# The rests of A as float16 against the bfloat16 upper halves of the weights, in the second product of a gated block

## The chip, the cores and the metric

The kernel runs on one core of a Trainium2 chip. The metric is the device time of one execution in microseconds (us). Before the change it is 698.72 us, the median of three runs (698.67 to 698.84).

## The reference

A block of two gated products over x (2 x 1024 tokens x 2048). The first multiplies the layer-normalised x, quantised to 8 bits, with a quantised context. The second multiplies the layer-normalised result with a 0/1 weight matrix of 2048 x 2048. Cut to what matters:

```python
x = x + tanh(g_xattn[0]) * matmul(fake_quant(layernorm(x)), fake_quant(ctx_4096))

y = layernorm(x)                                # 2 x 1024 x 2048
y_ei = concatenate([y[..., :1638], -4.0 * y[..., 1638:]], -1)
out = einsum('bsi,if->bsf', y_ei, kernel.astype(float32))   # kernel: 2048 x 2048, true or false
x = x + tanh(g_ffn[0]) * scale * out
```

Everything is float32 in the reference. The change concerns the second product alone.

## The kernel before

**Tiles and stages.** The 2048 tokens are 16 tiles of 128. The first half of the kernel's work on a batch (8 tiles) is the first product; its operands are small whole numbers held in float16 (matmuls at lines 544 and 646; line 574 makes a column sum of the context with a matrix of ones). The second product follows, batch by batch. It works on *pairs* of token tiles (p, 8 of them) as a 2 x 2 block product: A is split into four blocks (two token tiles, two halves of the 2048 inputs), the weights B into four blocks of 1024 x 1024, and a scheme with seven block products (M1 to M7) instead of eight combines sums and differences of the blocks. `ops_product2(q, ...)` handles two pairs at a time (q = 0 to 3), and for them goes through the seven products in the order of `ORDER`.

**One product for one pair.** The left block is 128 tokens x 1024 inputs, that is KH = 8 steps k of 128 inputs; the right block is 1024 wide, in two halves j of 512. To keep float32's accuracy the left block A is split in two:

- `part_hi` (line 738, ACT) copies A into a page of type fp32r, which keeps fewer bits of the fraction. This is `hi`.
- `part_lo` (line 742, DVE or POOL, as the planner chooses) takes the difference A - hi, also as fp32r. This is `lo`, the rest.

The weights lie in memory as bytes; `load_w` brings them in, and `widen` (line 782, ACT) turns 1024 of them per partition into fp32r, one page for each step k. They are whole numbers of small size.

`mm2` (line 809) then issues, for each k, four matmuls into the same accumulator in PSUM: hi with the left and the right half of the weights, lo with the left and the right half. The 128 x 128 piece of hi or lo is the stationary operand, which is loaded into TensorE's array before each matmul; the 512 columns of weights are the moving operand. There are 4 x 7 x 2 x 8 x 4 = 1,792 such matmuls, 896 with hi and 896 with lo. For an fp32r matmul the load of the stationary operand is part of the matmul instruction; for float16 it is an instruction of its own in TensorE's queue. The profile shows loads of both kinds as rows of the engine PEld.

After the last k of a product, `add2` (line 825, DVE) adds the accumulator, times the factor `f2`, onto the old x, and `store2` writes it out.

**Where A comes from.** `factor` (lines 447 to 461, DVE) makes one over the standard deviation for each tile; `scale2` (line 685, DVE) applies it; `turn2` (line 692, TensorE) transposes four pieces of 128 x 128 at a time, in float32, and `take2` copies them to A. `combine` (lines 722 to 728) forms the block sums.

**Order.** All engines' instructions are written out in an order that a planner makes: every piece of work is an `op` with a cost per engine, the buffers that it needs and a due time; `Plan.order` simulates them and keeps the best of two tries. TensorE's main work stands in a fixed order, and transposes and column sums are put in between. The two pairs of a product are staggered by LAG = 4 steps of k: four steps of the first pair, then steps of the two in turn, then four steps of the second.

Of the kernel before, what the change touches and what calls it, by code (L numbers as in the profile page):

```python
# [12 lines left out]
F32R = mybir.dt.float32r  # L13
F16 = mybir.dt.float16
BF = mybir.dt.bfloat16
# [3 lines left out]
ALU = mybir.AluOpType  # L19

P = 128
NB = 512
HB = 1024
EPS = 1e-5
UNIT = 2.0**-24
CENTER = 128.0
PAGES = 44

# [6 lines left out]
class Plan:  # L35
# [77 lines left out]
    def order(self, lag, start, runs, seed=1):  # L113


        self.dues()
        chance = random.Random(seed)
        free, count = dict(self.free), dict(self.count)
        dues = [o.due for o in self.ops]
        best = None  # L120
        for i in range(runs):
            self.free, self.count = dict(free), dict(count)
            try:
                end = self.run(lag, start)
            except RuntimeError:
                end = None
            if end is not None and (best is None or end <= best[0]):
                best = end, self.began, [o.engine for _, _, o in self.began]
                dues = [o.due for o in self.ops]
                held = self.held_up()  # L130
            for o, due in zip(self.ops, dues):
                o.due = due
            for ops in held:
                if chance.random() < 0.5:
                    step = chance.choice((3.0, 6.0, 12.0, 24.0))
                    for o in ops:
                        o.due -= step
            if i % 3:
                place = chance.uniform(0.0, self.place)
                for o in self.ops:  # L140
                    if o.place is None and abs(o.due - place) < 120.0 and chance.random() < 0.1:
                        o.due += chance.uniform(-25.0, 25.0)
        _, self.began, engines = best
        for (_, _, o), e in zip(self.began, engines):
            o.engine = e
        return [o for _, _, o in self.began]
# [133 lines left out]
def gated_xattn_ffn_kernel(  # L280
# [26 lines left out]

    nc = tc.nc  # L310
    B, S, D = x.shape
    K = kv.shape[1]
# [7 lines left out]
    KH = KT // 2  # L320
# [19 lines left out]
    def page(shape, dtype, name: str):  # L340
        return pages.tile([P] + shape, dtype, tag="page", name=name)
# [8 lines left out]
    sc = const.tile([P, 7], F32, name="sc")  # L350
    nc.sync.dma_start(sc, scalars.partition_broadcast(P))
    gate = const.tile([P, 2], F32, name="gate")
# [8 lines left out]
    c1 = const.tile([P, 1], F32, name="c1")  # L361
    nc.vector.tensor_scalar(c1, z1, -1.0, CENTER, ALU.mult, ALU.add)
    c2 = const.tile([P, 1], F32, name="c2")
# [3 lines left out]
    f1u = const.tile([P, 1], F32, name="f1u")  # L367
    nc.vector.tensor_scalar(f1u, f1, 1.0 / UNIT, None, ALU.mult)
    f1c1u = const.tile([P, 1], F32, name="f1c1u")
# [7 lines left out]
    nc.vector.tensor_scalar(kc12d, f1c1, c2, float(K), ALU.mult, ALU.mult)  # L377
    nc.vector.tensor_scalar(kc12, c1, -CENTER, None, ALU.add)
    nc.vector.tensor_scalar(kc12, kc12, f1c2, float(K), ALU.mult, ALU.mult)
    f2 = const.tile([P, 1], F32, name="f2")  # L380
    nc.vector.tensor_scalar(f2, gate[:, 1:2], sc[:, 6:7], None, ALU.mult)

    ident = const.tile([P, P], F32, name="ident")
    make_identity(nc, ident)
# [56 lines left out]
    def factor(v, t: int):  # L441


        va, sd = root.pop((v, t))
        mean = mv[v, t][:, 0:1]
        r0 = small.tile([P, 1], F32, tag="r0", name=f"r0_{v}{t}")
        nc.vector.reciprocal(r0, sd)

        e = small.tile([P, 1], F32, tag="e", name=f"e_{v}{t}")
        nc.vector.tensor_scalar(e, r0, r0, va, ALU.mult, ALU.mult)  # L450
        nc.vector.tensor_scalar(e, e, -0.5, 1.5, ALU.mult, ALU.add)
        r = small.tile([P, 1], F32, tag="r", name=f"r_{v}{t}", bufs=T)
        nc.vector.tensor_scalar(r, r0, e, None, ALU.mult)
        fac[v, t] = (r, mean)
        if v == "a":
            w = small.tile([P, 1], F32, tag="w", name=f"w_{v}{t}")
            nc.vector.tensor_scalar(w, va, r, zs1, ALU.mult, ALU.mult)
            nc.vector.tensor_scalar(w, w, mean, None, ALU.subtract)
            nc.vector.tensor_scalar(r, r, rs1, None, ALU.mult)
            wr = small.tile([P, 1], F32, tag="wr", name=f"wr_{v}{t}")  # L460
            nc.vector.tensor_scalar(wr, w, r, None, ALU.mult)
            fac[v, t] = (r, w, wr)
# [42 lines left out]
    def take1(t: int, h: int, engine=None):  # L505
# [5 lines left out]
        if engine == "ACT":  # L511
            nc.scalar.activation(dst, v, AF.Copy, bias=-CENTER)  # L512
        else:
            nc.vector.tensor_scalar(dst, v, -CENTER, None, ALU.add)  # L514

# [159 lines left out]
    A, hi, lo, wt, wb, wr, wf, back, acc2 = ({} for _ in range(9))  # L675
# [54 lines left out]
    def left(m: str, p: int):  # L730

        t, u = 2 * p, 2 * p + 1
        return {"M1": (t, 0), "M2": (t, 1), "M3": (t, 1), "M4": (u, 1), "M5": (u, 0),
                "M6": (t, 0), "M7": (p, "S3")}[m]
# [3 lines left out]
        nc.scalar.copy(hi[m, p], A[left(m, p)])  # L738

    def part_lo(m: str, p: int, engine=None):  # L740
        lo[m, p] = page([KH, P], F32R, f"lo_{m}_{p}")
        engines[engine].tensor_sub(lo[m, p], A[left(m, p)], hi[m, p].bitcast(F32))  # L742


# [51 lines left out]
    def apart(p: int, m: str):  # L796

        return p == T // 2 - 1 and SUM[m] == "Y"

    def mm2(q: int, m: str, p: int, k: int, js=(0, 1)):  # L800
        if m in OPENS and k == 0 and apart(p, m):
            acc2[SUM[m], p] = [ps_tr.tile([P, NB], F32, tag="tr", name=f"acc2_{m}_{p}_{j}") for j in range(2)]
        elif m in OPENS and k == 0:
            acc = ps_acc.tile([P, 2, NB], F32, tag="acc", name=f"acc2_{m}_{p}")
            acc2[SUM[m], p] = [acc[:, j, :] for j in range(2)]
            acc2[SUM[m], p, 0] = flat(acc)
        for part in (hi, lo):
            for j in js:
                nc.tensor.matmul(  # L809
                    acc2[SUM[m], p][j],  # L810
                    part[m, p][:, k, :],
                    wf[q, m, k][:, ts(j, NB)],
                    start=(m in OPENS and k == 0 and part is hi),
                    stop=(k == KH - 1 and part is lo),
                    skip_group_check=True,
                )
# [17 lines left out]
    def ops_norm(v: str, t: int, **when):  # L834
        name = lambda kind: ((kind + v, t), 0)
        op({"DVE": 2.0}, variance, v, t, writes=[name("v")], **when,
           reads=[(("bn" + v, t), c) for c in range(NC)])
        op({"ACT": 1.0}, square_root, v, t, reads=[name("v")], writes=[name("sd")], **when)
        op({"DVE": 8.0 if v == "a" else 4.0}, factor, v, t, reads=[name("sd")], writes=[name("r")], **when)
# [187 lines left out]
    def ops_parts(m: str, p: int):  # L1027
        a = ("A",) + left(m, p)
        op({"ACT": ACT(HB)}, part_hi, m, p, reads=both(a), writes=[(("hi", m, p), 0)],
           opens=[("page", ("hi", m, p))], lead=60)  # L1030
        op({"DVE": DV2(HB), "POOL": GPS(HB)}, part_lo, m, p, reads=[*both(a), (("hi", m, p), 0)],
           writes=[(("lo", m, p), 0)], opens=[("page", ("lo", m, p))], lead=60, port=True)
# [20 lines left out]
    def ops_product2(q: int, between):  # L1053
        pairs = (2 * q, 2 * q + 1)
        for n, m in enumerate(ORDER):
# [27 lines left out]
            for i, k, *js in steps:  # L1083
                p = pairs[i]
                js = js[0] if js else (0, 1)
                acc = ("acc2", SUM[m], p)
                two = apart(p, m)
                keys = [(acc + (j,), 0) if two else (acc, j) for j in js]
                opens = [("tr", acc + (j,)) for j in js] if two else [("acc", acc)]
                op({"PE": 2.1 * len(js)}, mm2, q, m, p, k, js, main=True, writes=keys,  # L1090
                   reads=[(("hi", m, p), 0), (("lo", m, p), 0), (("wf", q, m, k), 0)],
                   opens=opens if m in OPENS and k == 0 else [])
                if k == KH - 1:
                    for js2 in [(j,) for j in js] if two else [js]:
                        v = ("back", p) + TAKES[m]
                        keys = [(acc + (j,), 0) if two else (acc, j) for j in js2]
                        op({"DVE": DV2(len(js2) * NB)}, add2, m, p, js2, reads=keys, writes=[(v, j) for j in js2],
                           due=plan.place)
                        if m in LAST:
                            op({"SP": DMA}, store2, p, *TAKES[m], js2, reads=[(v, j) for j in js2], due=plan.place + 60)  # L1100
# [67 lines left out]
    for t in range(TPB, T):  # L1168
        v = ("x", t, 1)
# [60 lines left out]
```

## Time and profile before

| | |
|---|---|
| time, median of three | 698.72 us |
| time of the profiled execution | 698.79 us |
| its span in the profile | 697.0 us |
| granted TensorE clock | full |
| TensorE matmul busy | 674.0 us |
| TensorE weight load busy (beside the matmuls) | 471.7 us |
| VectorE (DVE) busy | 490.2 us |
| ScalarE (ACT) busy | 455.4 us |
| GpSimd (POOL) busy | 316.8 us |
| DMA | 155.78 MB |
| second product, first batch | about 145 to 367 us of the span |
| second product, second batch | about 476 to 693 us |

In a row of the profile's groups stand the line, the engine, the operation, the tile that it writes and those that it reads, the shape, the count, then the busy time, the mean length of one in ns, and the idle time of the engine before them with what ended it. Matmuls overlap: the length of one runs from its start to the end of its results, which is longer than the distance to the next one. The timeline gives start and length in us and an engine's row; neighbours of the same kind are merged (x2). In the chain of work that ended last each row has a start, a length and what ran.

### The profile page before, as it was taken

Reading aid. Unit: us, or ns where it says so; the run is one execution under the profiler, and the core shown is the slowest. Engines: PE = TensorE matmul, PEld = TensorE weight load, DVE = VectorE, ACT = ScalarE, POOL = GpSimd, SP = SyncE. Lnnn points to the kernel's source line nnn. Section 1 sums busy time; section 2 is a strip of 40 time slices with the busy share of each in tenths; the row PEclk is TensorE's granted clock in tenths of the full one; section 3 lists DMA queues with packets and bytes.
Section 4 is the critical chain, followed back from the end, with each engine's and each line's share of the span. In section 5 each row is a group of like instructions: output and inputs, shape, how many; then the busy total and the mean of one; then the engine's idle time right before and its main releaser. Section 6 shows DMA issues by size and latency. Waiting matters only on the chain.

```text
span 697.0 us, 8833 instructions
## 1 busy us (share of the span) xinstructions
PE 674.0 (97%) x3180; PEld 471.7 (68%) x3180; DVE 490.2 (70%) x717; ACT 455.4 (65%) x536; POOL 316.8 (45%) x210
## 2 busy tenths in 40 slices
PE   1999999989999999999999999999999999999997
PEld 0444444468788888878885444447888888888885
DVE  6899958899998886497878888468572425583331
ACT  4599444286888566699926768229699347689540
POOL 8166789863625221855717887975120101040000
PEclk9999999999999999999999999999999999999999
DMA  8999406777995799477379677327074379155032
GB/s 302 393 393 380 162 13 231 259 261 251 361 400 225 233 324 339 140 247 278 120 263 330 222 268 245 121 92 275 27 260 162 105 231 324 67 170 222 22 131 90
DMA packets 63580, 155.78 MB, mean 223 GB/s; under 512 B 4912, under 2 KB 21296, under 8 KB 63536
## 3 DMA queue, kind: packets, MB, share of 16 engines
q1 hardware_dynamic: 63536, 155.21, 62.9%
q8 instruction: 25, 0.41, 0.2%
q14 instruction: 19, 0.16, 0.1%
HBM read 117.44 MB, written 37.75 MB: 223 GB/s over the span
## 4 chain that ended last, share of the span: by engine, by line
PE 87%; DMA 4%; DVE 4%; POOL 2%; ACT 2%; issue 1%; SPq 0%; ACTq 0%; DVEq 0%
PE acc_M L809 57%; PE acc L544 19%; PE acc_M L646 7%; PE tr L692 4%; DMA kv<-in_kv_dram 3%; DMA x<-in_x_dram 1%; POOL x L596 1%; DVE wB L767 1%; ACT wf_M L782 1%; POOL x L592 1%; PE tr L503 1%; DVE qn L472 0%; PE cs L574 0%; DVE x L685 0%; DVE bn_b L426 0%
## 5 line engine op out<-in xcount | busy, mean ns | idle before, releaser
L809 PE MATMUL acc_M<-wf_M,hi_M 128*128 128x512 f32 x896 | 282.0, 395 | 1.6 <-ACT wf_M L782 1.5
L809 PE MATMUL acc_M<-wf_M,lo_M 128*128 128x512 f32 x896 | 277.6, 390 | 0.6 <-POOL lo_M L742 0.6
L782 ACT ACTIVATE wf_M<-wr_M 128x1024 fp32r<-128x1024 uint8 x224 | 221.6, 1050 | 26.8 <-DMA wr_M<-in_wmask_dram 24.2
L809 PEld LDWEIGHTS acc_M<-wf_M,lo_M 128*128 128x128 f32 x896 | 168.0, 188 | 36.8 <-POOL lo_M L742 1.3
L809 PEld LDWEIGHTS acc_M<-wf_M,hi_M 128*128 128x128 f32 x896 | 164.1, 188 | 34.4 <-ACT wf_M L782 3.2
L544 PE MATMUL acc<-q,q1T 128*128 128x512 f16 x768 | 171.6, 381 | 1.2 <-DVE q1T L514 0.8
L825 DVE SCALAR_TENSOR_TENSOR back<-acc_M,f,back 128x1024 f32<-128x1024 f32 (+1 forms) x58 | 72.1, 1245 | 124.7 <-PE acc_M L809 117.1
L742 POOL TENSOR_TENSOR lo_M<-A,hi_M 128x1024 fp32r<-128x1024 f32 x24 | 62.1, 2586 | 179.5 <-ACT hi_M L738 160.1
L544 PEld LDWEIGHTS <-q1T 128*128 128x128 f16 x768 | 75.2, 98 | 90.2 <-issue 1.9
L592 POOL TENSOR_TENSOR x<-x,row 128x512 f32<-128x512 f32 x64 | 88.6, 1408 | 43.8 <-ACT sd_a L438 15.5
L596 POOL TENSOR_TENSOR x<-x,e 128x512 f32<-128x512 f32 x64 | 92.0, 1458 | 30.6 <-ACT e L586 16.1
L738 ACT CAST hi_M<-A 128x1024 fp32r<-128x1024 f32 x48 | 50.1, 1044 | 13.1 <-POOL A L726 4.7
L530 ACT ACTIVATE q<-kv,sc,rs 128x1024 uint8<-128x1024 f32 x45 | 53.5, 1236 | 7.8 <-DMA kv<-in_kv_dram 5.1
L586 ACT ACTIVATE e<-acc,tokb,f1u 128x512 f32<-128x512 f32 x34 | 25.1, 774 | 49.6 <-PE acc L544 47.8
L426 DVE BATCH_NORM_STATS2 bn_b<-x 128x6 f32<-128x512 f32 x64 | 43.1, 684 | 15.9 <-POOL x L596 15.6
L495 ACT COPY A<-tr 128x512 f32<-128x512 f32 x35 | 20.3, 584 | 46.5 <-PE tr L692 45.8
L742 DVE TENSOR_TENSOR lo_M<-A,hi_M 128x1024 fp32r<-128x1024 f32 x24 | 33.7, 1421 | 7.2 <-ACT hi_M L738 7.2
L568 DVE TENSOR_TENSOR pair<-pair,q 128x1024 f16<-128x1024 f16 x36 | 36.6, 1022 | 2.5 <-ACT q L530 0.8
L728 POOL TENSOR_TENSOR A<-A,A 128x1024 f32<-128x1024 f32 x8 | 21.1, 2648 | 23.7 <-DVE A L726 16.4
L522 POOL MEMSET q<- 128x1024 f32 x32 | 29.2, 952 | 5.1 <-DVE q L532 2.2
L512 ACT ACTIVATE q1T<-tr 128x1024 f16<-128x1024 uint8 x22 | 21.3, 1019 | 7.5 <-PE tr L503 6.8
L767 DVE SCALAR_TENSOR_TENSOR wB<-wB,wB 128x2048 uint16<-128x2048 uint16 x8 | 24.2, 3031 | 0.0
(103 smaller groups left out, 594.1 us busy)
## 6 DMA issues: line engine op xcount, KB each, us to landing
kv<-in_kv_dram SPq DMA_DIRECT2D x64, 512.0 KB, 9.2
x<-in_x_dram SPq DMA_DIRECT2D x32, 512.0 KB, 7.7
x<-x SPq DMA_DIRECT2D x32, 512.0 KB, 3.0
back<-x SPq DMA_DIRECT2D x32, 512.0 KB, 6.1
wr_M<-wt_T SPq DMA_DIRECT2D x32, 512.0 KB, 5.6
out_dram<-back SPq DMA_DIRECT2D x30, 512.0 KB, 3.6
wr_M<-in_wmask_dram SPq DMA_DIRECT2D x24, 512.0 KB, 5.4
n<-in_x_dram SPq DMA_DIRECT2D x16, 512.0 KB, 7.2
```

The costliest lines, as they stand in the source:

```text
L426: nc.vector.bn_stats(bn[v, t][:, c, :], xt[src[v, t, c // 2]][:, ts(c % 2, NB)])
L530: nc.scalar.activation(low, v, AF.Identity, bias=z2, scale=rs2)
L544: nc.tensor.matmul(acc1[b, c, tiles[0]][:, i, :], q1T[tiles[i]][:, k, :], rhs1(b, c, k), start=(k == 0), stop=(k == KT - 1),)
L568: nc.vector.tensor_add(colsum[b, c], colsum[b, c], v[:, i : i + 2, :])
L592: nc.gpsimd.tensor_add(xc, xc, colrow[b, c])
L596: nc.gpsimd.tensor_add(xc, xc, ev.pop((t, c)))
L646: nc.tensor.matmul(acc1[key][:, i, :], left_half(p, LEFT1[m])[:, 4 * s + k, :], right1(m, h, s)[:, k, :], start=(m in OPENS and s == 0 and ...
L738: nc.scalar.copy(hi[m, p], A[left(m, p)])
L742: engines[engine].tensor_sub(lo[m, p], A[left(m, p)], hi[m, p].bitcast(F32))
L782: nc.scalar.activation(wf[q, m, k], wr[q, m, k // 4][:, k % 4, :], AF.Copy, bias=-float(RIGHT[m][1]))
L809: nc.tensor.matmul(acc2[SUM[m], p][j], part[m, p][:, k, :], wf[q, m, k][:, ts(j, NB)], start=(m in OPENS and k == 0 and part is hi), stop= ...
L825: nc.vector.scalar_tensor_tensor(v, acc, f2, v, ALU.mult, ALU.add)
```

## The change

`lo` becomes a page of float16, in `part_lo`. Its matmuls no longer read the widened weights as fp32r but the upper 16 bits of each as bfloat16, that is every second 16-bit element of the same page. The hi matmuls stay as they were. So that the small rests lie in float16's range, A is scaled by 2^19 in the factor of the second normalisation (`factor`, for v = "b"), and `f2` is divided by 2^19. In the planner, a list is given a first value; no cost is changed.

```diff
+BIG = 2.0**19
...
-        best = None
+        best, held = None, []
...
-    nc.vector.tensor_scalar(f2, gate[:, 1:2], sc[:, 6:7], None, ALU.mult)
+    nc.vector.tensor_scalar(f2, gate[:, 1:2], sc[:, 6:7], 1.0 / BIG, ALU.mult, ALU.mult)
...
-        nc.vector.tensor_scalar(e, e, -0.5, 1.5, ALU.mult, ALU.add)
+        big = BIG if v == "b" else 1.0
+        nc.vector.tensor_scalar(e, e, -0.5 * big, 1.5 * big, ALU.mult, ALU.add)
...
     def part_lo(m: str, p: int, engine=None):
-        lo[m, p] = page([KH, P], F32R, f"lo_{m}_{p}")
+        lo[m, p] = page([KH, P], F16, f"lo_{m}_{p}")
         engines[engine].tensor_sub(lo[m, p], A[left(m, p)], hi[m, p].bitcast(F32))
...
-        for part in (hi, lo):
+        w = wf[q, m, k]
+
+        upper = w.bitcast(BF).rearrange("p (n b) -> p n b", b=2)[:, :, 1]
+        for part, rhs in ((hi, w), (lo, upper)):
             for j in js:
                 nc.tensor.matmul(
                     acc2[SUM[m], p][j],
                     part[m, p][:, k, :],
-                    wf[q, m, k][:, ts(j, NB)],
+                    rhs[:, ts(j, NB)],
                     start=(m in OPENS and k == 0 and part is hi),
```

In the new file line 809 is line 817, and line 742 is line 747.

## The prediction

> **What bounds the kernel now.** First the page's busy shares and the chain that ended last:
>
> ```profile
> PE 674.0 (97%) x3180; PEld 471.7 (68%) x3180; DVE 490.2 (70%) x717; ACT 455.4 (65%) x536; POOL 316.8 (45%) x210
> PE 87%; DMA 4%; DVE 4%; POOL 2%; ACT 2%; issue 1%; SPq 0%; ACTq 0%; DVEq 0%
> PE acc_M L809 57%; PE acc L544 19%; PE acc_M L646 7%; PE tr L692 4%; DMA kv<-in_kv_dram 3%; DMA x<-in_x_dram 1%; POOL x L596 1%; DVE wB L767 1%; ACT wf_M L782 1%; POOL x L592 1%; PE tr L503 1%; DVE qn L472 0%; PE cs L574 0%; DVE x L685 0%; DVE bn_b L426 0%
> ```
>
> TensorE makes 87% of the chain, and line 809, the line of the change, 57% of the span, 397 us. Then the groups:
>
> ```profile
> L809 PE MATMUL acc_M<-wf_M,hi_M 128*128 128x512 f32 x896 | 282.0, 395 | 1.6 <-ACT wf_M L782 1.5
> L809 PE MATMUL acc_M<-wf_M,lo_M 128*128 128x512 f32 x896 | 277.6, 390 | 0.6 <-POOL lo_M L742 0.6
> L809 PEld LDWEIGHTS acc_M<-wf_M,lo_M 128*128 128x128 f32 x896 | 168.0, 188 | 36.8 <-POOL lo_M L742 1.3
> L544 PE MATMUL acc<-q,q1T 128*128 128x512 f16 x768 | 171.6, 381 | 1.2 <-DVE q1T L514 0.8
> L544 PEld LDWEIGHTS <-q1T 128*128 128x128 f16 x768 | 75.2, 98 | 90.2 <-issue 1.9
> ```
>
> The two matmul groups of line 809 wait only 1.6 + 0.6 us in all, so the stage is bound by how fast TensorE strings its matmuls together. The means of 395 and 381 ns are latencies that overlap; the price of a matmul is the distance to the next. From the chain in order of time:
>
> ```profile
> 439.29 29.35 PE acc L544 x136
> 506.40 70.77 PE acc_M L809 x312
> 615.45 77.13 PE acc_M L809 x340
> ```
>
> float16: 29.35 / 136 = 215.8 ns each. fp32r: 70.77 / 312 = 226.8 and 77.13 / 340 = 226.9 ns. Over all 1,792 matmuls of line 809 the distances in the records average 227.7 ns once the six real stalls (over 250 ns) are left out; the 0.9 ns above 226.8 sit in some ten matmuls after each stall or transpose (230 to 236 ns), 1.8 us in all.
>
> **The change, part by part.** The programs built from both versions carry the same work in the same order on every engine and queue, with the same number of waits: planner costs are untouched and the extra `held = []` only matters if a first plan fails. One thing differs: each of the 896 `lo` matmuls now has a weight load that is an instruction of its own, as line 544 has; an fp32r matmul has its load built in.
>
> *The bare widths.* 896 `lo` matmuls from 226.8 to 215.8 ns would take off 896 x 11.0 = 9.9 us (9.7 with 226.7 and 215.9; I use 9.7). All of it would lie on the path: the waits of line 809 are 2 us, and the second batch's first product, which follows at 367 us, waits 0.3 us once (line 646 for ACT).
>
> *The joint between the two kinds.* After the change, every k step of a pair runs hi, hi, lo, lo: fp32r, fp32r, f16, f16, 448 such groups. The trace of before holds this pattern once, where the column sum of line 574 stands inside the second product (TensorE's rows, then its weight loads; start and length in us):
>
> ```profile
> 351.07 0.62 PE L809 MATMUL acc_M<-wf_M,hi_M 128*128 128x512 f32 x2
> 351.52 0.61 PE L809 MATMUL acc_M<-wf_M,lo_M 128*128 128x512 f32 x2
> 351.98 0.61 PE L574 MATMUL cs<-pair,ones_h 128*128 128x512 f16 x2
> 352.24 0.81 PE L809 MATMUL acc_M<-wf_M,hi_M 128*128 128x512 f32 x2
> 352.89 0.62 PE L809 MATMUL acc_M<-wf_M,lo_M 128*128 128x512 f32 x2
> ```
>
> ```profile
> 351.30 0.41 PEld L809 LDWEIGHTS acc_M<-wf_M,lo_M 128*128 128x128 f32 x2
> 351.98 0.12 PEld L574 LDWEIGHTS <-ones_h 128*128 128x128 f16 x2 [0.26 <-issue]
> 352.21 0.41 PEld L809 LDWEIGHTS acc_M<-wf_M,hi_M 128*128 128x128 f32 x2
> ```
>
> From 351.98 to 352.89, two f16 and two fp32r matmuls take 0.91 us. Two and two at their own widths would be 0.432 + 0.454 = 0.886; four fp32r take 0.907. So the joint eats what the narrower matmuls give. The weight loads say where: an fp32r load starts together with the matmul before it, while the f16 load waits until the last fp32r matmul has streamed (351.98, the very start of its own matmul). In the records' nanosecond stamps the ends of the matmuls (start plus length) follow each other by 232 and 216 (f16), then 229, 233, 231, 227 (fp32r). The other joint of this kind, from line 809 into line 646 at 366.95 us, gives the same 232, then 215 and 216. A new group is thus 232 + 216 + 229 + 233 = 910 ns, against 4 x 227.7 = 910.8 on average now: 448 x (910 - 910.8) = -0.4 us.
>
> Here the Trainium skill speaks otherwise. "TensorE: Matmul & The Clock Gate", in its spec table and in "Architectural detail", has the queue pull weight loads ahead of matmuls in flight; "Weight-path perf modes" has the load fast for 128 columns of a type other than FP32. The fast load shows (98 against 188 ns). By the pulling ahead, f16 behind fp32r would cost 216, and the sum would be the 9.7 us of the bare widths. The two joints measured show no pulling ahead of a separate load past an fp32r matmul, so I take 910. Bounds: if the fp32r pair keeps to an undisturbed 227, the group is 232 + 216 + 227 + 227 = 902 (-3.9 us); if the first f16, coming after a disturbed fp32r matmul, takes the 238 ns that is the worst seen after a transpose, it is 916 (+2.3 us).
>
> *The moving operand at every second bfloat16.* No TensorE row of before reads with a step. The nearest is the fp32r row itself: it streams the same 2 KB per partition in 226.8 ns, so a step of two need not cost more than that, 11 ns over the contiguous f16. Bounds: 0, by the page "SBUF — State Buffer", section Door 1, whose rule is that at least two hits on a 16-byte line are read at full bandwidth (here four); and, if only half of the columns came per cycle, as much again as a matmul, 896 x 0.213 = 191 us. I take 0: bytes and lines are the fp32r row's, and 2 KB in 227 ns was shown.
>
> *Line 742, the rest in float16.* 24 on POOL at 2,586 ns, 24 on DVE at 1,421, and 8 more. The inputs stay f32, so I take no change. Half the written bytes might save some (the f16-only DVE sums of lines 628 and 630 take 1.05 to 1.49 us for the same 1,024 elements); a dearer conversion could cost. Cover: POOL waits 160.1 us at this line for the hi copies, and TensorE waits 0.6 + 1.3 us for lo. Without that cover, each 0.1 us more costs at most 56 x 0.1 = 5.6 us, which needs every one on the path.
>
> *The rest*: the scaling by 2^19 rides on instructions that exist (one more scalar in f2, about 0.2 us at the start, used only from the first add of the second product on; other constants in line 451). Pages, DMAs and buffers are the same in number. 896 further instructions for TensorE's queue: line 544 issues two per 216 ns without a gap, so 0.
>
> **Sum**: -0.4 us. On the profiled execution (698.79 us, span 697.0) 698.4; on the median of 698.72, **698.3 us**. From the bounds of the joint and line 742, 694.5 to 701.5 is this case's own range.
>
> **Rivals.** *The load is pulled ahead after all, or a regular pattern of four settles in a better phase*: 2 x 226.8 + 2 x 216 a group, -9.7 us, 689.0; anything between that and -1.4 belongs here. For it: f16 to f16, transposes (f32, load built in) into f16 and f16 into transposes cost no extra in this trace. Against: both joints from fp32r into f16 cost 16 ns. *The step of two costs on top of the joint* (the other side): each lo matmul streams like an fp32r one, +11 ns, group 932: 448 x 21 = +9.5 us, **708.2**. It decides once a stepped read costs more than about 4 ns a matmul (896 x 4 = 3.6 us, beyond the joint's own spread). For it: the 11 ns of fp32r may come from reading four bytes a column, and a stepped read touches the same bytes; against: the same 11 ns may belong to the built-in load. At half rate this rival is 889 us. *The change doesn't do what it says*: excluded as far as the build tells, since the lo loads have become separate instructions.
>
> **How the numbers follow.** A group is known to about 6 ns either way; 0.2% (1.4 us) is 3.1 ns a group and about what a measurement of this kernel can tell from no change. Near-cancelling: 0.48, of which 0.12 faster, 0.24 same, 0.12 slower. Pulled ahead or a better phase: 0.27, faster. Stepped read dearer: 0.20, of which 0.03 at half rate. Joint worse than 916: 0.05. Together 0.39 faster, 0.24 same, 0.37 slower. The range leaves out about one in ten at each end: 692 to 707.
>
> **What would show it.** Right: lo loads at about 98 ns that start with their own matmul after each fp32r pair; groups of four 0.91 us apart in the long stretches; the chain still 57% line 809, with stretches of over 300 matmuls at 227 to 228 ns on average. Pulled ahead: lo loads that start with the second hi matmul, 0.89 us a group. Stepped read: the distance from the first to the second lo matmul at 227 ns or more instead of 216. The prediction is wrong if that distance, or the first lo's 232, does not recur, or if lo on POOL or DVE takes long enough for line 817's matmuls (809 before) to wait on it.

## The result and the profile after

The changed kernel takes 706.60 us (median; 706.53 to 706.73), the kernel before 698.69 us beside it: ratio 1.0113 (95% interval 1.0096 to 1.0131), 7.9 us slower. The forecast was 698.3 us, no change to speak of.

From the page of the changed kernel, the busy shares and the groups of the change's line (809 before, 817 now):

```profile
PE 682.0 (97%) x3180; PEld 355.4 (50%) x3180; DVE 495.5 (70%) x717; ACT 455.4 (65%) x536; POOL 315.7 (45%) x210
PE 89%; DVE 5%; DMA 3%; POOL 2%; issue 1%; ACT 1%; SPq 0%; ACTq 0%; DVEq 0%
L817 PE MATMUL acc_M<-wf_M,hi_M 128*128 128x512 f32 x896 | 363.8, 487 | 1.4 <-ACT wf_M L787 1.4
L817 PE MATMUL acc_M<-wf_M,lo_M 128*128 128x512 bf16 x896 | 281.0, 393 | 0.6 <-POOL lo_M L747 0.6
L817 PEld LDWEIGHTS <-lo_M 128*128 128x128 f16 x896 | 52.1, 98 | 123.4 <-issue 121.1
```

The shares of the engines other than the weight loads are the same, and the two matmul groups again wait next to nothing (1.4 + 0.6 us), so no new wait and no other engine has taken over. TensorE's weight loads fell by 116 us, and it did not help: they had been covered. The 487 ns of a hi matmul are no price either; half of these rows start in the records about 190 ns earlier than the others, in the middle of the matmul before, and last 580 ns instead of 390, while the distances between the ends of the matmuls hardly differ. The price is in the chain in order of time:

```profile
510.58 72.30 PE acc_M L817 x312
621.55 78.84 PE acc_M L817 x340
```

That is 231.7 and 231.9 ns a matmul where 226.8 and 226.9 stood, 927 ns for a group of hi, hi, lo, lo instead of 907. Over all matmuls of the line, with the real stalls over 250 ns left out, the distances average 232.6 ns (227.7 before), or 930.4 a group against 910.9: 448 x 19.5 = 8.7 us. The stalls themselves are 0.9 us shorter. That leaves 7.8 us; the spans in the profiles differ by 7.8 us (704.8 against 697.0), the medians by 7.9.

One stretch of the timeline of the changed kernel, TensorE's rows and then its weight loads:

```profile
519.24 0.62 PE L817 MATMUL acc_M<-wf_M,lo_M 128*128 128x512 bf16 x2
519.50 0.82 PE L817 MATMUL acc_M<-wf_M,hi_M 128*128 128x512 f32 x2
520.16 0.62 PE L817 MATMUL acc_M<-wf_M,lo_M 128*128 128x512 bf16 x2
520.42 0.83 PE L817 MATMUL acc_M<-wf_M,hi_M 128*128 128x512 f32 x2
521.09 0.63 PE L817 MATMUL acc_M<-wf_M,lo_M 128*128 128x512 bf16 x2
```

```profile
519.23 0.12 PEld L817 LDWEIGHTS <-lo_M 128*128 128x128 f16 x2 [0.27 <-issue]
519.48 0.41 PEld L817 LDWEIGHTS acc_M<-wf_M,hi_M 128*128 128x128 f32 x2
520.15 0.12 PEld L817 LDWEIGHTS <-lo_M 128*128 128x128 f16 x2 [0.26 <-issue]
```

And from the waits of the weight loads (us in total, times, longest us):

```profile
PEld L817 <- issue: 121.1, 446, 0.3
```

The lo loads do start only with their own matmul (519.23 and 519.24), as at the joint shown before; the idle time of 0.27 us before them recurs 446 times. But in the records' nanosecond stamps the ends of the four matmuls follow each other, on average over all groups, by 231 and 233 ns (hi) and 240 and 227 ns (lo), where 229, 233, 232 and 216 were taken. The hi pair is as forecast; both lo matmuls are dearer, the first by 8 ns and the second by the 11 ns that the rival of the stepped read had given.

### The profile page after: what moved, and what is told of

It is laid out like the page before. It is cut to its first block, busy times and chain, and to the rows that moved or that the text cites. A ratio compares the mean times of both kernels' runs of the same rounds, so it can differ in the third digit from the quotient of the medians.

```text
span 704.8 us, 8833 instructions
## 1 busy us (share of the span) xinstructions
PE 682.0 (97%) x3180; PEld 355.4 (50%) x3180; DVE 495.5 (70%) x717; ACT 455.4 (65%) x536; POOL 315.7 (45%) x210
## 4 chain that ended last, share of the span: by engine, by line
PE 89%; DVE 5%; DMA 3%; POOL 2%; issue 1%; ACT 1%; SPq 0%; ACTq 0%; DVEq 0%
PE acc_M L817 59%; PE acc L549 19%; PE acc_M L651 7%; PE tr L697 4%; DMA x<-in_x_dram 2%; DMA kv<-in_kv_dram 1%; POOL x L601 1%; DVE wB L772 1%; DVE bn_a L430 1%; POOL x L597 1%; PE tr L508 1%; DVE qn L477 0%; PE cs L579 0%; DVE x L690 0%; DVE bn_b L430 0%
## 5 line engine op out<-in xcount | busy, mean ns | idle before, releaser
L817 PE MATMUL acc_M<-wf_M,hi_M 128*128 128x512 f32 x896 | 363.8, 487 | 1.4 <-ACT wf_M L787 1.4
L817 PE MATMUL acc_M<-wf_M,lo_M 128*128 128x512 bf16 x896 | 281.0, 393 | 0.6 <-POOL lo_M L747 0.6
L747 POOL TENSOR_TENSOR lo_M<-A,hi_M 128x1024 f16<-128x1024 f32 x24 | 61.2, 2550 | 180.5 <-ACT hi_M L743 170.1
L817 PEld LDWEIGHTS <-lo_M 128*128 128x128 f16 x896 | 52.1, 98 | 123.4 <-issue 121.1
L573 DVE TENSOR_TENSOR pair<-pair,q 128x1024 f16<-128x1024 f16 x36 | 40.7, 1135 | 1.7
L747 DVE TENSOR_TENSOR lo_M<-A,hi_M 128x1024 f16<-128x1024 f32 x24 | 35.5, 1496 | 6.5 <-ACT hi_M L743 6.5
L517 ACT ACTIVATE q1T<-tr 128x1024 f16<-128x1024 uint8 x22 | 21.3, 1019 | 7.6 <-PE tr L508 6.6
```

What stands on the lines that cost most here:

```text
L573: nc.vector.tensor_add(colsum[b, c], colsum[b, c], v[:, i : i + 2, :])
L817: nc.tensor.matmul(acc2[SUM[m], p][j], part[m, p][:, k, :], rhs[:, ts(j, NB)], start=(m in OPENS and k == 0 and part is hi), stop=(k == KH ...
```

## The experiments

Three causes could make lo dear: the step of two in what it reads (*step*), the change of kind between fp32r and float16 (*joint*), or float16 multiplied with bfloat16 (*types*). Times below are medians, ratios against the kernel before on the same chip (698.8 us).

**No step.**

```diff
-        upper = w.bitcast(BF).rearrange("p (n b) -> p n b", b=2)[:, :, 1]
+        upper = w.bitcast(BF)[:, 0:HB]
```

> The lo matmuls read 512 neighbouring bfloat16 elements of the widened page instead of every second one, so they multiply with the wrong values; number, order and types of all instructions stay. If the step of two costs (each lo matmul 227 instead of 216 ns, the first one 239 instead of 232), a group of four falls from 927 to about 910 ns and the time to about 699 us. If the change of kind alone costs, the group stays at 927 ns and the time at 706.6 us.

Measured: 697.66 us, ratio 0.9985 (0.9978 to 0.9991). The chain and the timeline of this run:

```profile
506.25 71.24 PE acc_M L817 x312
615.36 76.60 PE acc_M L817 x340
520.26 0.61 PE L817 MATMUL acc_M<-wf_M,lo_M 128*128 128x512 bf16 x2
520.52 0.81 PE L817 MATMUL acc_M<-wf_M,hi_M 128*128 128x512 f32 x2
521.18 0.61 PE L817 MATMUL acc_M<-wf_M,lo_M 128*128 128x512 bf16 x2
```

From one lo pair to the next it is 0.92 us here, 0.91 on average over all matmuls (909.1 ns a group). By kind: 228 and 232 ns (hi), 232 and 216 (lo). The step was worth 8.9 us; without it the time is about a microsecond below that of before, close to the forecast.

The 909 ns are the average of two steady patterns, though. In the first stretch shown a matmul takes 228.3 ns (71.24 / 312), or 913 a group, with 228, 236, 233 and 215 in the stamps; in the second it takes 225.3 (76.60 / 340), or 901 a group, with 227, 226, 231 and 216, so that the hi pair is undisturbed. What decides between the two is not known. The second lo matmul takes 227 ns with the step in both of these stretches and 215 to 216 without, so its 11 ns do not depend on the pattern.

**One type, and an even start.** Two edits of the same line, the step kept: the halves read as float16, or the lower halves instead of the upper.

```diff
-        upper = w.bitcast(BF).rearrange("p (n b) -> p n b", b=2)[:, :, 1]
+        upper = w.bitcast(F16).rearrange("p (n b) -> p n b", b=2)[:, :, 1]     # first
+        upper = w.bitcast(BF).rearrange("p (n b) -> p n b", b=2)[:, :, 0]      # second
```

> The same stepped 16-bit halves are read as float16 instead of bfloat16, so that both operands of a lo matmul are of one type; the values are then wrong. If mixing float16 with bfloat16 costs, the second lo falls to 216 ns and the time by some 10 us to about 697 us; by the step and by the change of kind it stays at 706.6 us.

> The lower instead of the upper halves are read, at the same step of two but from a start that is a multiple of four bytes; they are zeros, so lo adds nothing. If the odd start of the upper half makes the price, the second lo falls to 216 ns and the time to about 698 us; if the step does, it stays at 706.6 us.

Measured: 706.77 us (1.0114, 1.0097 to 1.0131) and 706.71 us (1.0113, 1.0099 to 1.0127). Both equal the change. Neither the mixture of types nor the odd start costs anything here; nor do the values read matter, since the lower halves are zeros.

**No change of kind, step kept.** hi is float16 as well, so its loads are instructions of their own like lo's.

```diff
-BIG = 2.0**19
+BIG = 2.0**8
...
-        hi[m, p] = page([KH, P], F32R, f"hi_{m}_{p}")
+        hi[m, p] = page([KH, P], F16, f"hi_{m}_{p}")
...
-        engines[engine].tensor_sub(lo[m, p], A[left(m, p)], hi[m, p].bitcast(F32))
+        engines[engine].tensor_sub(lo[m, p], A[left(m, p)], hi[m, p])
...
-        for part, rhs in ((hi, w), (lo, upper)):
+        for part, rhs in ((hi, upper), (lo, upper)):
```

> hi becomes float16 too (A scaled by 2^8 instead of 2^19), and both hi and lo read the upper halves at every second element: no change of kind is left, every matmul is stepped. If the step costs 11 ns a matmul, a group is 4 x 227 = 908 ns, about as before the change: 697 to 699 us. If the step is free and the change of kind costs all, a group is 4 x 216 = 864 ns: 698.7 - 448 x 0.047 = about 677.6 us.

Measured: 695.02 us, ratio 0.9946 (0.9931 to 0.9961); 903.7 ns a group, 226 ns for each matmul:

```profile
503.88 70.46 PE acc_M L817 x312
612.05 76.80 PE acc_M L817 x340
```

The step alone, in a stream with no joint, takes a float16 matmul from 216 to 226 ns. This is within 1 ns the price of an fp32r matmul, which passes over the same 2 KB per partition. The time is 2 us below what was expected, for two reasons of about the same size: a matmul takes 1 ns less than the undisturbed 226.8 of fp32r, and the float16 stream has none of the slow matmuls (230 to 236 ns) that fp32r shows after a transpose.

**Larger steps.** The same kernel with every third and every fourth element.

```diff
-        upper = w.bitcast(BF).rearrange("p (n b) -> p n b", b=2)[:, :, 1]
+        upper = w.bitcast(BF)[:, 0:3 * NB].rearrange("p (n b) -> p n b", b=3)[:, :, 1]    # three
+        upper = w.bitcast(BF).rearrange("p (n b) -> p n b", b=4)[:, :, 1]                 # four
...
-                    rhs[:, ts(j, NB)],
+                    rhs,
```

> As the float16 runs with a step of two (226 ns a matmul) and of four (451 ns), now with a step of three, 3 KB a partition; columns are wrong. If the price goes with the bytes passed over, 339 ns a matmul: 695.0 + 1,792 x 0.113 = about 897 us. If it goes in powers of two, or by whether a step is above two, 451 ns and 1,097 us.

> As the run with float16 hi and lo and a step of two, but every fourth 16-bit element is read, over twice the bytes; columns are then wrong. If the step's price grows with the bytes passed over, a matmul takes 236 ns or more and the time is 695.0 + 1,792 x 0.010 = 713 us or more. If any step costs the same 10 ns, it stays at 695 us.

Measured: 890.96 us (1.2751, 1.2725 to 1.2776) and 1,097.1 us (1.5699, 1.5677 to 1.5720). From the chains, step three and then step four:

```profile
612.40 105.04 PE acc_M L817 x312
770.25 114.48 PE acc_M L817 x340
```

```profile
727.94 140.92 PE acc_M L817 x312
937.39 153.58 PE acc_M L817 x340
```

Per matmul 336.7 and 451.7 ns, after 225.8 at a step of two. The times stand as 2 to 2.98 to 4.00: about 113 ns for each KB that the 512 columns pass over, with 216 ns as the floor for a contiguous 1 KB. With every step up to four each 16-byte line that is passed over is also read, so these runs do not tell bytes from lines; a step of eight was not run.

**fp32r over fewer bytes.** If bytes set the price, fp32r's own 227 ns should fall with them. In the kernel before:

```diff
-                    wf[q, m, k][:, ts(j, NB)],
+                    wf[q, m, k][:, j * NB : j * NB + NB // 2].unsqueeze(2).to_broadcast([P, NB // 2, 2]),
```

> The kernel before the change, but each fp32r matmul of the second product takes 256 of the 512 weight columns and reads each of them twice in succession: type and number stay, the bytes passed over fall from 2 KB to 1 KB; the columns are then wrong. If the fp32r matmul's 227 ns come from 2 KB a partition, as the stepped float16 reads suggest, it falls to about 216 ns: 698.7 - 1,792 x 0.011 = about 679 us. If they come from the weight load that is built into the instruction, it stays at 698.7 us.

Measured: 681.14 us, ratio 0.9748 (0.9731 to 0.9764). The chain of this run:

```profile
497.94 67.34 PE acc_M L809 x312
601.66 73.40 PE acc_M L809 x340
```

215.8 and 215.9 ns: fp32r with its built-in load runs at float16's pace as soon as it passes over 1 KB. The slow matmuls after transposes are gone too (average over all 215.9). So the 11 ns never belonged to the load.

**Fewer changes of kind.** In the changed kernel the order of hi and lo is turned round from group to group, except at the first k; once with the step and once without.

```diff
+    last_kind = []
...
-        for part, rhs in ((hi, w), (lo, upper)):
+        both_kinds = [(hi, w), (lo, upper)]
+        if k > 0 and last_kind and last_kind[0] is lo:
+            both_kinds.reverse()
+        last_kind[:] = [both_kinds[1][0]]
+        for part, rhs in both_kinds:
...
-                    start=(m in OPENS and k == 0 and part is hi),
-                    stop=(k == KH - 1 and part is lo),
+                    start=(m in OPENS and k == 0 and part is both_kinds[0][0]),
+                    stop=(k == KH - 1 and part is both_kinds[1][0]),
```

> From group to group the order of hi and lo is turned round (hi hi lo lo, lo lo hi hi), except at the first k of a product: 248 changes from hi to lo instead of 452, step kept. If the change of kind makes all of the 42 ns that a group (927) stands above its bare widths (885), 0.45 of them go: 19 ns a group, 8.5 us, about 698.1 us. If the step makes 22 of them and the change of kind 20, 9 ns a group go: about 702.6 us.

> Order turned round from group to group, and neighbouring bfloat16 elements read (wrong values for lo): the change of kind alone, at 0.55 of its number. With the step away a group was 909 ns, 24 above the bare 885; 0.45 of 24 is 11 ns a group, 4.8 us below the 697.7 of that run: about 692.9 us. If the change of kind does not cost, 697.7 us.

Measured: 703.19 us (1.0063, 1.0048 to 1.0078) with the step, 695.96 us (0.9959, 0.9946 to 0.9973) without. The first lies by the step's forecast of 702.6. The second saves 1.7 us of the 4.8 expected: a group is 903.8 ns, 19 above the bare widths instead of 13. In the records the entry into float16 costs 232 ns and the next 216 as ever, and it comes half as often; but the fp32r matmuls, now four in a row, stay at 230 to 232 ns. Part of the joint's price is thus not paid at the first float16 matmul but by the fp32r matmuls. Why they stay slow for a while is open.

**Without either.** hi and lo are float16 and the widened weights too; nothing of the computation is left out. Against the changed kernel:

```diff
-BIG = 2.0**19
+BIG = 2.0**8
...
-        hi[m, p] = page([KH, P], F32R, f"hi_{m}_{p}")
+        hi[m, p] = page([KH, P], F16, f"hi_{m}_{p}")
...
-        engines[engine].tensor_sub(lo[m, p], A[left(m, p)], hi[m, p].bitcast(F32))
+        engines[engine].tensor_sub(lo[m, p], A[left(m, p)], hi[m, p])
...
-        wf[q, m, k] = page([HB], F32R, f"wf_{q}_{m}_{k}")
+        wf[q, m, k] = page([HB], F16, f"wf_{q}_{m}_{k}")
...
-        upper = w.bitcast(BF).rearrange("p (n b) -> p n b", b=2)[:, :, 1]
-        for part, rhs in ((hi, w), (lo, upper)):
+        for part, rhs in ((hi, w), (lo, w)):
```

> hi and lo are float16 and the weights are widened to float16 pages that both read without a step: no step, no change of kind. If these two are all that stands between a matmul and 216 ns, a group is 4 x 216 = 864 ns against 903.7 in the run with float16 and a step of two, 448 x 0.040 = 18 us less than its 695.0: about 677 us. If the 226 ns come from something else (the order, the waits), it stays at about 695 us.

Measured: 679.40 us, ratio 0.9722 (0.9709 to 0.9736), faster than both kernels. From its chain and its waits (TensorE; total us, times, longest us):

```profile
496.04 67.34 PE acc_M L816 x312
599.72 73.40 PE acc_M L816 x340
...
PE acc_M L816 <- ACT wf_M L787: 3.4, 4, 1.4
```

A group is 864 ns, as expected: 448 x (910.9 - 863.9) = 21.1 us off. Measured are 19.4; TensorE now waits 3.4 us for the widening where it waited 1.5, which is the rest.

## Why the prediction was wrong

- *What bounds the kernel*: right. The stretches of line 809 set the time before and after, and waits did not move it.
- *The bare widths*: the figures hold (float16 216, fp32r 227), their reading does not. The 11 ns between them are the price of 2 KB instead of 1 KB, not of the type or its load, and the change keeps lo at 2 KB.
- *The joint*: right on average, with some luck. A group without the step measures 909.1 ns against the 910 taken from one place in the trace, and its kernel 697.66 us against 698.3. But no long stretch ran at 910: one ran at 913, and one at 901, which is the lower bound of 902 (an undisturbed fp32r pair). The rule of loads pulled ahead of matmuls in the Trainium skill ("TensorE: Matmul & The Clock Gate", "Architectural detail") does not hold behind an fp32r matmul here: 446 times in the changed kernel the load began late.
- *The moving operand at every second bfloat16*: this is the step that failed. It took 0 from the Trainium skill's rule of two hits on a 16-byte line ("SBUF — State Buffer", Door 1) and took 11 ns as the most that the step need cost, though the row named as nearest, fp32r over the same 2 KB, stood at 227 ns. That row's price was the answer: (930.4 - 909.1) / 2 = 10.7 ns a lo matmul, 448 x 21.3 = 9.5 us by groups, 8.9 us between the two runs. "2 KB in 227 ns was shown" was read as "no dearer than fp32r", when it had to be read as "no cheaper". At a step of four, which still has two elements in each 16-byte line, a matmul takes 451.7 ns: two hits on a line are not enough for this operand. The same sentence of the page says that each access that crosses to a new line pays a penalty, and the prediction left that half out; above the floor of 216 ns the times do rise with the lines crossed, as they do with the bytes. (The upper bound of 191 us for half rate was worked out with 213 ns a matmul; with the 216 measured at line 544 it is 193.)
- *Line 742 in float16*: right. The median of one is 2,404 ns on POOL and 1,218 on DVE, where it was 2,410 and 1,220, and TensorE waits 0.6 us for lo as before.
- *The rivals*: the stepped read on top of the joint, 708.2 us at a chance of 0.20 (0.03 of it for half rate), is what happened, with its sign (second lo at 227 ns) as it was written. The measured 706.6 lies at the very end of the stated range of 692 to 707, which reached so far only because of this rival; the case's own range ended at 701.5. The load that is pulled ahead did not occur. Its -9.7 us is measured from an undisturbed group of four fp32r matmuls (907.2 ns); from the 910.8 that the main sum uses, the same group gives -11.3 us.

## What to carry to other kernels

Price the moving operand by the bytes that its 512 columns pass over, not by its type or the bytes that it uses: a 16-bit view of 32-bit data keeps the 32-bit price, and the steps of three and four cost in proportion. When a row of the trace with the same access stands there, take its price and not a rule's. Two kinds of matmuls in turn cost about as much as the narrower kind gives back (909.1 ns a group without the step, 910.9 before); one narrow kind throughout gave 2.8% here.

## What was not expected of the hardware

- fp32r matmuls over 1 KB of moving data run at 215.9 ns, as float16 does. Their 226.8 ns over 2 KB fit the same 113 ns per KB as float16 at steps of two, three and four.
- A float16 weight load behind an fp32r matmul starts only when that matmul has streamed, in nearly every group of the changed kernel. The first float16 matmul then takes 232 ns instead of 216, though the load itself is given as 98 ns. That the late load makes these 16 ns is likely but not shown for fp32r. In the kernel before, a float16 load behind a float32 transpose (load built in as well, 128 columns) starts 107 ns ahead of its own matmul, and that matmul takes 215 or 216 ns.
- After a transpose, fp32r matmuls over 2 KB run at 230 to 236 ns for up to ten matmuls. With 1 KB of data they do not.
- Hi, hi, lo, lo without the step settles for tens of microseconds in one of two patterns, 913 or 901 ns a group. What selects the pattern is open.
